# Layer 2's clamp moved from VectorE to GpSimd, its subtraction into a bias on ScalarE, in a four-layer graph network

## The chip, the cores and the metric

The kernel runs on one core of a Trainium2 chip. Its engines are named as in the profile: PE (TensorE, matrix products), DVE (VectorE), ACT (ScalarE), POOL (GpSimd) and SP (SyncE, which only issues transfers here). Each has its own queue and works through it in order; semaphores tie the queues together. The time is the device time of one execution in microseconds, and the lower the better. A profile is one execution on its own, with a span from its first to its last record.

## The reference, cut to what matters

There are 4096 nodes with 64 features and a dense 4096 x 4096 matrix `adj`. Four layers follow each other. Each normalises the rows of `x`, applies relu, aggregates over `adj` in its own way, and adds to `x`. Layer 0 is a plain product, layer 1 attention with a sigmoid, layer 3 a weighting by rank. Layer 2, which is changed, aggregates logarithmic maps on the Poincare ball:

```python
def _logmap(x, y, c):
    sub = _mobius_add(-x, y, c)
    sub_norm = jnp.maximum(jnp.linalg.norm(sub, axis=-1, keepdims=True), MIN_NORM)
    ...
    arg = jnp.clip(sqrt_c * sub_norm, 0.0, TANH_CLIP)
    return 2.0 / (sqrt_c * lam_x) * jnp.arctanh(arg) * sub / sub_norm
...
deg = jnp.maximum(adj.sum(axis=1, keepdims=True), 1e-08)
w = adj / deg
log_ij = _logmap(x[:, None, :], x[None, :, :], c)
agg = jnp.einsum('ij,ijc->ic', w, log_ij)
```

The kernel never forms the 4096 x 4096 x 64 array. For each pair of nodes it computes one number, the hyperbolic distance divided by its hyperbolic sine, multiplies it by `adj`, and sums with a matrix product. With u the scaled hyperbolic cosine that comes out of PE, and SC a power of two that scales it, that number needs u squared less a quarter of SC squared (the squared sine), kept above zero, its square root, its inverse root, and the logarithm of cosine plus root.

## The kernel before, in words

**Tiling.** A work item of layer 2 is a tile of 128 partitions by 2 x 512 elements: two chunks of 128 source nodes against a block of 512 target nodes. The scaled distance is symmetric, so only blocks on and above the diagonal are computed, and blocks above it are also transposed on PE and used a second time ("two"). That makes 72 items in 8 rows of blocks, with 16, 14, 12 and so on down to 2 items; in 8 of the 72, on the diagonal, only half of the tile is needed ("cut"), 128 by 512 elements.

**One item, step by step.** Each step is a generator named `l2_...` (lines 1005 to 1212); the profile's names are those of the tiles.
- `l2_dists` on PE: two float32 products (`mm<-RT,LT`) and two bf16 ones (`mm<-RB,LB`) put u into a PSUM tile. There are two such tiles, so that the distances of item k+2 wait until item k's has been read.
- `l2_squares` on ACT: `v<-mm`, v is u squared.
- `l2_clamps` on DVE: `v<-v`, subtract and keep above a floor, in one instruction with two operations.
- `l2_signs` on PE: a last small product turns u in PSUM into its absolute part.
- `l2_roots` on ACT: Ln of v in place (`v<-v`), Exp with scale 0.5 into t (`t<-v`), Exp with scale -0.5 in place (`v<-v`): root and inverse root.
- `l2_coshs` on DVE: `t<-mm,t`, cosine plus root. This frees the PSUM tile.
- `l2_logs` on ACT: `t<-t`, the second Ln.
- `l2_pairs` on DVE: `t<-t,v`, distance times inverse root.
- `l2_weights` on DVE: `w<-t,adj`; `l2_turns` on PE: `tr<-ident,t`; `l2_weights2` on DVE: `w<-tr,adj`, twice per item.
- `l2_sums` and `l2_sums2` on PE: `acc<-w,HA`, 512 columns wide for the item itself, 256 wide for its transposed use; `l2_gathers` adds the transposed sums into `others`.

The tiles v and t come from one pool of six buffers, so three items can be under way.

**The epilogue of a row.** When a row's last item is summed, `after2` and `before3` (lines 613 and 532) follow for its 512 nodes: two transposes, a product, and some two dozen short instructions on DVE, with copies on ACT, a power on POOL for the norm (`r_nn`), one for the normalisation of layer 3 (`ln_r`), and the addition of a bias on POOL (`x<-x,b`).

**What sets the order.** The order of every queue is fixed when the program is built. `in_turn` (line 712) keeps a set of threads; each offers the engine of its next instruction and the time at which a small model, `Pace` (line 59), thinks that it can start, and the earliest goes next. `Pace.cost` (line 76) prices each instruction. `in_steps` (line 1214) ties several steps to a fixed order: for the item number k of each round it issues its stages one after another, each with an offset ("behind"), so that -1 means the next item and 1 the one before. Layer 2's ACT steps are one such group, its PE steps another, and its DVE steps a third. A changed price moves instructions in all layers, since every thread is planned by the same model.

**The first half of the program** (layers 0 and 1, up to about 482 us) reads `adj` twice, 512 KB at a time, over SP's queue. Layer 0's first products wait for the normalised rows HA, which pass through DVE, ACT, and a power on POOL; between them DVE adds up degrees (`dg<-dg,adj`). Small constants (`later_constants`) are made on POOL and DVE at about 35 to 43 us.

## Time and profile before

| | us |
|---|---|
| median of 3 runs | 1199.96 (1198.93 to 1201.73) |
| the profiled execution | 1194.61 |
| its span | 1192.9 |
| layer 2, about 482 to 957 | 475 |
| PE busy in it | 417.7 |
| DVE busy in it | 435.6 |
| ACT busy in it | 374.2 |
| POOL busy in it | 33.5 |

The profiled execution ran 5.4 us below the median. In the lines of the profile L129 is a helper that records every instruction, so instructions are known by their tiles. A line of a group gives its engine, operation, written tile, read tiles and shape, then the count, the busy time in us and the mean of one in ns, and after the last bar the idle time of that engine just before these instructions and what ended it. A line of the timeline gives start, duration, engine and instruction, with the idle time before it in brackets. A line of the waits gives who waited for whom, us in total, number of times, and the longest. In a table by stretches each engine has its busy time and its instructions, followed by PE's granted clock, the busy share of the transfer engines and GB/s.

### The profile page before, as it was taken

Reading aid. Unit: us, or ns where it says so; the run is one execution under the profiler, and the core shown is the slowest. Engines: PE = TensorE matmul, PEld = TensorE weight load, DVE = VectorE, ACT = ScalarE, POOL = GpSimd, SP = SyncE. Lnnn points to the kernel's source line nnn. Section 1 sums busy time; section 2 is a strip of 40 time slices with the busy share of each in tenths; the row PEclk is TensorE's granted clock in tenths of the full one; section 3 lists DMA queues with packets and bytes.
Section 4 is the critical chain, followed back from the end, with each engine's and each line's share of the span. In section 5 each row is a group of like instructions: output and inputs, shape, how many; then the busy total and the mean of one; then the engine's idle time right before and its main releaser. Section 6 shows DMA issues by size and latency. Waiting matters only on the chain.

```text
span 1192.9 us, 15567 instructions
## 1 busy us (share of the span) xinstructions
PE 1074.0 (90%) x5367; PEld 443.4 (37%) x5392; DVE 954.1 (80%) x1595; ACT 780.4 (65%) x1250; POOL 121.5 (10%) x99
## 2 busy tenths in 40 slices
PE   4799999999999999899979979899879679999997
PEld 1234443333333333244434434344433323333332
DVE  6888888869988988798999999898989884555550
ACT  1055456677767767879888788787877554555554
POOL 3122321102000010000010010100010130000000
PEclk9998999999999999899999999999999889999999
DMA  8899999865767775544535435354444297888830
GB/s 303 290 409 366 400 384 337 301 216 193 246 230 247 254 247 170 194 141 159 194 106 184 169 119 197 108 161 157 159 151 166 94 396 292 316 311 315 308 112 9
DMA packets 77190, 271.75 MB, mean 228 GB/s; under 512 B 10040, under 2 KB 11064, under 8 KB 77112
## 3 DMA queue, kind: packets, MB, share of 16 engines
q1 hardware_dynamic: 75456, 270.57, 63.9%
q8 instruction: 42, 0.69, 0.2%
q10 hardware_dynamic: 1656, 0.20, 0.1%
q14 instruction: 36, 0.29, 0.1%
HBM read 269.68 MB, written 1.05 MB: 227 GB/s over the span
## 4 chain that ended last, share of the span: by engine, by line
PE 48%; DVE 26%; ACT 11%; issue 7%; DMA 5%; POOL 2%; ACTq 0%; SPq 0%; DVEq 0%; POOLq 0%
PE acc L129 23%; PE mm L129 16%; PE tr L129 9%; DVE t L129 6%; DVE w L129 6%; DMA adj<-in_adjT_dram 4%; DVE dg L129 3%; ACT wt L129 3%; ACT v L129 2%; DVE v L129 2%; ACT t L129 1%; DVE sig L129 1%; ACT sig L129 1%; POOL lo_s L129 1%; ACT lo_sq L129 1%
## 5 line engine op out<-in xcount | busy, mean ns | idle before, releaser
L129 PE MATMUL acc<-w,HA 128*65 128x256 f32 (+1 forms) x736 | 251.8, 478 | 32.0 <-DVE w L129 23.7
L129 ACT ACTIVATE v<-v 128x1024 f32<-128x1024 f32 (+1 forms) x144 | 145.3, 1009 | 62.1 <-DVE v L129 59.8
L129 ACT ACTIVATE wt<-mm 128x1024 uint16<-128x1024 f32 x124 | 120.5, 1020 | 98.6 <-PE mm L129 98.6
L129 ACT ACTIVATE sig<-mm,att_b,att_a 128x1024 f32<-128x1024 f32 x128 | 148.3, 1201 | 40.9 <-PE mm L129 39.8
L129 DVE TENSOR_TENSOR sig<-sig,adj 128x1024 f32<-128x1024 f32 x128 | 152.2, 1219 | 25.5 <-ACT sig L129 25.2
L129 PE MATMUL acc<-adj,HA 128*64 128x512 f32 x512 | 128.8, 636 | 25.0 <-DVE HA L129 21.4
L129 DVE TENSOR_TENSOR dg<-dg,adj 128x1024 f32<-128x1024 f32 x114 | 139.1, 1220 | 2.0 <-DMA adj<-in_adjT_dram 0.6
L129 PEld LDWEIGHTS acc<-w,HA 128*65 128x65 f32 x736 | 95.2, 140 | 121.0 <-issue 58.7
L129 PE MATMUL mm<-qT,kT 64*128 64x512 f32 x512 | 129.5, 619 | 3.3 <-ACT sig L129 3.3
L129 PE MATMUL acc<-sig,HL 128*64 128x512 f32 x512 | 123.3, 604 | 1.6 <-DVE sig L129 1.5
L129 PE MATMUL acc<-wt,S 128*64 128x512 bf16 (+1 forms) x479 | 97.5, 388 | 3.0 <-issue 2.7
L129 DVE SCALAR_TENSOR_TENSOR t<-t,v 128x1024 f32<-128x1024 f32 x72 | 83.3, 1157 | 4.1 <-ACT t L129 4.1
L129 DVE SCALAR_TENSOR_TENSOR t<-mm,t 128x1024 f32<-128x1024 f32 x72 | 83.3, 1156 | 3.9 <-ACT t L129 2.1
L129 DVE TENSOR_TENSOR w<-tr,adj 128x512 f32<-128x512 f32 x120 | 78.1, 682 | 8.7 <-PE tr L129 8.7
L129 DVE TENSOR_TENSOR w<-t,adj 128x1024 f32<-128x1024 f32 x72 | 83.5, 1159 | 1.2
L129 PE MATMUL mm<-RT,LT 64*128 64x512 f32 (+1 forms) x288 | 78.8, 624 | 3.6 <-DVE t L129 3.6
L129 PE MATMUL tr<-ident,t 128*128 128x128 f32 x480 | 66.3, 279 | 17.0 <-DVE w L129 7.9
L129 ACT ACTIVATE t<-t 128x1024 f32<-128x1024 f32 x72 | 72.1, 1002 | 13.4 <-DVE t L129 13.2
L129 DVE TENSOR_SCALAR RT<-adj 128x1024 bf16<-128x1024 f32 x74 | 50.0, 689 | 32.2 <-PE mm L129 31.8
L129 ACT ACTIVATE t<-v 128x1024 f32<-128x1024 f32 x72 | 72.7, 1010 | 2.3
L129 PEld LDWEIGHTS mm<-qT,kT 64*128 64x128 f32 x512 | 43.1, 185 | 74.2 <-ACT sig L129 35.2
L129 ACT ACTIVATE v<-mm 128x1024 f32<-128x1024 f32 x72 | 69.2, 962 | 0.8 <-PE mm L129 0.8
(206 smaller groups left out, 1287.3 us busy)
## 6 DMA issues: line engine op xcount, KB each, us to landing
adj<-in_adjT_dram SPq DMA_DIRECT2D x512, 512.0 KB, 4.7
x<-in_x_dram SPq DMA_DIRECT2D x4, 256.0 KB, 4.1
out_dram<-h SPq DMA_DIRECT2D x8, 128.0 KB, 2.5
b<-in_b_dram ACTq DMA_DIRECT2D x2, 32.0 KB, 5.7
W<-in_W_dram ACTq DMA_DIRECT2D x3, 16.0 KB, 3.9
W0T<-in_W0T_dram ACTq DMA_DIRECT2D x2, 16.0 KB, 5.5
W1T<-in_W1T_dram ACTq DMA_DIRECT2D x1, 16.0 KB, 4.9
W1T<-in_b_dram ACTq DMA_DIRECT2D x1, 0.2 KB
```

Of the source, the lines that this page charges most:

```text
L129: done = self.tc.keep_in_program_order(getattr(self.engine, op)(*args, **kw))
```

## The change

The clamp becomes a single maximum on POOL: v is kept at or above the next number over a quarter of SC squared. The subtraction goes into the first logarithm on ACT, as a bias held in a new constant tile `minus`. That logarithm is a step of its own, `l2_first_logs`. ACT's group is put into another order: first logarithm of item k, square of item k+1, the two exponentials of k, second logarithm of k (before, the second logarithm of k-1 came first, and the square of k+1 last). The clamps leave DVE's group and are a thread of their own on POOL. The planner's price of a POOL instruction other than a power or a tiny one changes from 0.3 + n/600 to 0.25 + n/300 us.

```diff
-V_MIN = 2.0**-64
+HALF = 0.25 * SC * SC
...
-            return 1.65 if ALU.pow in kw.values() or n <= 8 else 0.3 + n / 600
+            return 1.65 if ALU.pow in kw.values() or n <= 8 else 0.25 + n / 300
...
+    minus = const.tile([P, 1], F32, name="minus")
+    POOL.memset(minus, -HALF)
...
     def l2_clamps():
         for d in work:
-            yield "DVE", lambda: d.get("square")
+            yield "POOL", lambda: d.get("square")
             v = part(d, d["v"])
-            DVE.tensor_scalar(v, v, -half, V_MIN, ALU.add, ALU.max)
+            POOL.tensor_scalar(v, v, HALF * (1.0 + 2.0**-23), None, ALU.max)
             d["clamped"] = pace.latest
...
+    def l2_first_logs():
+        for d in work:
+            yield "ACT", lambda: latest(d.get("clamped"), opened.get("tables"))
+            v = part(d, d["v"])
+            ACT.activation(v, v, AF.Ln, bias=minus)
+            d["first_log"] = pace.latest
+
     def l2_roots():
         for k, d in enumerate(work):
             yield "ACT", lambda: latest(
-                d.get("clamped"), opened.get("tables"),
+                d.get("first_log"),
                 l1[2 * k + 1 - SIG].get("summed") if 2 * k < SIG else 0.0,
                 ago(work, k, SIG // 2, "weighed"), ago(work, k, SIG // 2, "turned"),
             )
             d["t"] = pair_buffer("t")
+            ACT.activation(part(d, d["t"]), part(d, d["v"]), AF.Exp, scale=0.5)
+            d["root"] = pace.latest
             v = part(d, d["v"])
-            ACT.activation(v, v, AF.Ln)
-            ACT.activation(part(d, d["t"]), v, AF.Exp, scale=0.5)
-            d["root"] = pace.latest
             ACT.activation(v, v, AF.Exp, scale=-0.5)
             d["inverse"] = pace.latest
...
-        in_steps((l2_logs(), 1, once), (l2_roots(), 0, once), (l2_squares(), -1, once)),
         in_steps(
-            (l2_clamps(), 0, once), (l2_pairs(), 1, once), (l2_weights(), 1, once),
+            (l2_first_logs(), 0, once), (l2_squares(), -1, once), (l2_roots(), 0, once), (l2_logs(), 0, once),
+        ),
+        in_steps(
+            (l2_pairs(), 1, once), (l2_weights(), 1, once),
             (l2_coshs(), 0, once), (l2_weights2(), 1, lambda d: 2 if d["two"] else 1 if d["first"] else 0),
         ),
-        l2_gathers(), l3_weights(), l3_pass(), l3_counts(), l3_masks(),
+        l2_clamps(), l2_gathers(), l3_weights(), l3_pass(), l3_counts(), l3_masks(),
```

More of the change, by code (lines that the diff above doesn't have):

```diff
@@ L943, in l1_sums @@
                 follow(with_mark(2, ib, after1(ib, acc, st), before2(ib, st)), ON_S, evicts=True)
-    half = 0.25 * SC * SC
     top = 2.0 * math.atanh(TANH_CLIP)
```

## The prediction

> **What bounds the kernel now.** I read the page's shares, then engine busy time by stretches, then one step of layer 2 in order of time, then the waits.

> ```profile
> span 1192.9 us, 15567 instructions
> PE 1074.0 (90%) x5367; PEld 443.4 (37%) x5392; DVE 954.1 (80%) x1595; ACT 780.4 (65%) x1250; POOL 121.5 (10%) x99
> ```

> PE is busiest and POOL nearly empty. The average mixes three stages; clamps exist only in layer 2, from 482 to about 957 us.

> ```profile
> core 0: us, PE busy (x) PEld busy (x) DVE busy (x) ACT busy (x) POOL busy (x), PEclk, DMA share, GB/s
> 545.00:595.00 50.00, 48.59 (x236) 23.62 (x233) 45.96 (x56) 44.36 (x51) 0.00 (x0) 1.00 0.52 179
> 595.00:625.00 30.00, 24.39 (x109) 11.05 (x108) 27.22 (x46) 23.90 (x29) 4.71 (x3) 0.94 0.33 106
> 770.00:800.00 30.00, 24.89 (x120) 11.38 (x116) 29.09 (x41) 24.07 (x27) 2.17 (x2) 1.00 0.44 145
> ```

> Inside a row of blocks (first stretch) PE is full. Where one row ends and the next begins (the other two) the row's epilogue lands on DVE, and DVE leads: 27.2 and 29.1 of 30 us against PE's 24.4 and 24.9. Over 482 to 957 the same view gives PE 417.7, DVE 435.6, ACT 374.2, POOL 33.5 of 475.0 us. One inner step:

> ```profile
> 565.76 0.68 DVE L129 TENSOR_SCALAR v<-v 128x1024 f32<-128x1024 f32 x1
> 566.48 1.06 ACT L129 ACTIVATE v<-v 128x1024 f32<-128x1024 f32 x1 [0.76 <-DVE v L129]
> 566.60 1.13 PE L129 MATMUL mm<-RT,LT 64*128 64x512 f32 x4
> 567.66 0.40 PE L129 MATMUL mm<-RB,LB 32*128 32x512 bf16 x4
> 567.99 1.94 PE L129 MATMUL acc<-w,HA 128*65 128x256 f32 x8
> 568.75 1.22 DVE L129 SCALAR_TENSOR_TENSOR t<-mm,t 128x1024 f32<-128x1024 f32 x1
> 569.77 1.04 PE L129 MATMUL tr<-ident,t 128*128 128x128 f32 x8
> 570.40 1.29 DVE L129 TENSOR_TENSOR w<-tr,adj 128x512 f32<-128x512 f32 x2 [0.43 <-PE tr L129]
> 570.64 1.88 PE L129 MATMUL acc<-w,HA 128*65 128x512 f32 x4
> 571.61 0.68 DVE L129 TENSOR_SCALAR v<-v 128x1024 f32<-128x1024 f32 x1
> ```

> Clamp to clamp is 5.85 us. PE's pieces follow without a gap: 1.06 + 0.33 + 1.78 + 0.87, and 1.81 for the sum ahead, 5.85. DVE spends 0.43 of it waiting for PE. So a clamp taken off DVE gains nothing in an inner step. The waits show where it can:

> ```profile
> ACT v L129 <- DVE v L129: 59.8, 60, 3.7
> PE acc L129 <- DVE w L129: 23.7, 22, 2.2
> ```

> ACT waits 59.8 us in all for clamps queued behind other DVE work, PE 23.7 us for DVE's weights. The chain of waits holds the clamp (DVE v) for 1.6% of the span, 19 us.

> **Prices.** POOL never ran this operation; the nearest rows, grouped by shape:

> ```profile
> L129 DVE TENSOR_SCALAR v<-v 128x1024 f32<-128x1024 f32 x64 | 43.7, 683 | 7.2 <-ACT v L129 7.2
> L129 POOL TENSOR_TENSOR x<-x,b 128x256 f32<-128x256 f32 x8 | 7.2, 903 | 0.0
> L129 DVE SCALAR_TENSOR_TENSOR hb<-ln_xc,ln_r 128x256 f32<-128x256 f32 x8 | 7.4, 925 | 0.4 <-POOL ln_r L129 0.3
> L129 DVE SCALAR_TENSOR_TENSOR h<-ln_xc,ln_r 128x256 f32<-128x256 f32 x16 | 6.7, 418 | 1.4 <-POOL ln_r L129 1.4
> L129 POOL MEMSET rb<- 128x512 f32 x2 | 1.0, 523 | 0.0
> masks.py:102 POOL TENSOR_SCALAR_AFFINE_SELECT near_f<-near_f 128x128 f32<-128x128 f32 x1 | 0.3, 306 | 0.0
> ```

> A 1-element memset is 0.11 us, so the memset slope is (523-105)/511 = 0.82 ns per element: lower bound 0.11 + 0.84 = 0.95 us for 1024. The one-input select, (306-105)/128 = 1.57 ns, gives 1.7. The two-input add, (903-105)/256 = 3.1 ns, gives 3.3, the upper bound from rows. Spans on POOL are rough[...], and the planner's new price is 3.66 us.

> [...]hb, alongside the POOL add, took 925 ns against 418 for the same shape alone. [...]sigmoid with two took 1201 ns, the relu with none 1020, so about 90 each. I take 1.7 to 2.5 us for the clamp, with 0.95 and 4 as ends.

> **The change, part by part.**

> *Off DVE:* 64 x 0.683 + 8 x 0.414 = 47.0 us. DVE falls from 435.6 to about 389.

> *On ACT:* the first Ln gets a bias pointer, 72 x 0.09 = 6.5 us. No activation is added. The second Ln now follows its own step's two exponentials, and must wait for cosh on DVE (1.22 plus handovers, about 1.4) which only the inverse exponential (1.08) covers: about 0.3 us a step. An ACT loop is then 1.18 + 0.95 + 1.09 + 1.4 + 1.05 = 5.67 us, under PE's 5.85. ACT effectively needs 374 + 6.5 + 20 = 401.

> *On POOL:* 72 clamps, 2 us each 144; with 33.5 of powers and adds, far from full. New wait: square, POOL, first Ln. Between square k+1 and first Ln k+1 ACT runs exponential, inverse, wait, second Ln of k: 1.09 + 1.4 + 1.05 = 3.5 us. That hides the clamp. Behind it on POOL stand the row's powers (2.5 and up to 1.9 us) and the 0.9 add; the exponential of the row's norm on ACT waits for the first.

> [...]DVE's pairs and weights read two SBUF tensors, 2.44 us a step, back to back. By the order of both queues the clamp becomes ready near the weights' end[...] and has 5.85 - 2.44 = 3.4 us before the next pairs.[...]

> *Row changes:* ACT no longer queues behind the epilogue. DVE's 435.6 of 475 was 92% full; with PE's 417.7 the largest and ACT at 401 and DVE at 389 close behind, I fill to 90%: 464, so -11. Ends: 0, and 417.7/0.92 = 454, -21.

> *Start of layer 2:* the eviction of layer 1's last sum now stands ahead of the first Ln, which moves from 484.9 to about 486.3: +1.

> *Layers 0 and 1:* the repriced POOL (and one new memset) reorders the plan. Two more degree adds stand ahead of the first normalised rows on DVE: 2 x 1.22 = 2.4 us later than 12.5, and PE idles until then. The eighth normalisation goes behind the constants: 37.9 becomes about 40.5. Later degree adds come earlier by as much, so I take +1, ends -3 and +5. DMA issue keeps the same 512 loads; layer-2 loads stay in the same pairs, layer 3 does the same work on PE.

> Sum: -11 + 1 + 1 = -9 on the profiled execution's 1194.6 (span 1192.9 and 1.7 around it): 1185.6. The median of the runs lies 5.4 above that execution, so 1191.

> **Rivals.** *B, [...]a slow clamp (slower).* Place: each inner step. Step = 2.44 + clamp. From 3.4 us on it decides. At 3.66 it is 6.10, +0.25 x about 45 inner steps = 11, less 5 at row changes and with the +2 above: 1208. At 4 us the same sum gives 1223. For: the hb row and the two-input slope. Against: one input only. *C, ACT takes the bound over:* row changes add copies of 3.9 us per row to an ACT loop of 5.67, so five steps need 32 where DVE took about 32; gain eaten, 1200. Against: copies can fill the 0.3 us waits. *D, the early reorder persists:* +5 or more through the load-bound start with a small gain in layer 2: 1206. That the clamps stay on DVE is excluded by the queue orders: POOL issues 72 of them.

> **How the numbers follow.** A 0.52, B 0.22, C 0.16, D 0.10. Within 0.2% (2.4 us, about what a measurement of this kernel can tell from none) lie 0.01 of A, 0.02 of B, 0.09 of C: 0.12. Slower: 0.01, 0.18, 0.07, 0.10: 0.36. Faster: 0.50 of A and 0.02 of B: 0.52. Range 1181 (all of the 90-to-92% fill) to 1213 (B up to 3.8 us); A alone 1183 to 1196.

> **What would show it.** Right: clamp spans of 1 to 3 us on POOL, inner steps still 5.85 with PE gapless, ACT's wait for the clamp small, row stretches shorter, pairs and weights still 1.22. Wrong: ACT first Ln waiting for POOL each step; pairs stretched beyond 1.22[...]; step at 2.44 + clamp; first PE matmul well after 15.4 us with the shift still present at 482.

## The result and the profile after

| | before | after |
|---|---|---|
| median of 4 runs, us | 1200.85 (1198.93 to 1202.79) | 1186.58 (1185.22 to 1186.75) |
| the profiled execution, us | 1194.61 | 1186.61 |
| its span, us | 1192.9 | 1184.6 |

The ratio is 0.9879, 95% interval 0.986 to 0.9898: the change makes the kernel 1.2% faster. The predicted time was 1191, its range 1181 to 1213.

The shares on the page of the changed kernel:

```profile
span 1184.6 us, 15638 instructions
...
PE 1078.5 (91%) x5367; PEld 449.7 (38%) x5392; DVE 929.3 (78%) x1523; ACT 783.1 (66%) x1250; POOL 324.3 (27%) x172
```

The 72 clamps have gone from DVE to POOL, which is now busy for 203 us more. DVE, however, lost only 24.9 us (954.1 to 929.3), where the clamps alone were 47.0. The rest is taken up below.

The changed kernel by stretches, the same three as before:

```profile
core 0: us, PE busy (x) PEld busy (x) DVE busy (x) ACT busy (x) POOL busy (x), PEclk, DMA share, GB/s
545.00:595.00 50.00, 50.00 (x245) 24.67 (x245) 43.23 (x49) 45.67 (x50) 23.37 (x10) 1.00 0.54 192
595.00:625.00 30.00, 26.08 (x114) 11.68 (x112) 26.12 (x42) 23.82 (x31) 17.94 (x8) 0.94 0.34 126
770.00:800.00 30.00, 27.30 (x121) 12.68 (x119) 28.16 (x38) 24.17 (x28) 18.50 (x8) 0.94 0.44 154
```

Inside the first row PE is full, as it nearly was. At the two row changes PE is busy for 1.7 and 2.4 us more, and DVE for about 1 us less. In the last stretch the granted clock was 0.94 in the mean, where it had been 1.00 (0.50 from 775.42 to 778.84 us). By busy time times one minus the clock, an estimate from this trace, that is 1.7 of the 2.4 us.

The clamp on POOL and the first logarithm, in the changed kernel's groups by shape:

```profile
L129 POOL TENSOR_SCALAR v<-v 128x1024 f32<-128x1024 f32 x64 | 187.2, 2925 | 194.8 <-ACT v L129 190.4 <-DVE w L129 4.0 <-ACT r_c L129 0.4
...
L129 ACT ACTIVATE v<-v,minus 128x1024 f32<-128x1024 f32 x64 | 72.7, 1137 | 7.8 <-POOL v L129 7.7
```

A clamp takes 2.93 us in the mean, against 0.68 on DVE. ACT waits only 7.7 us for all of them. The waits of the changed kernel, from 482 to 957 us:

```profile
DVE t L129 <- ACT t L129: 44.8, 41, 3.4
...
ACT t L129 <- DVE t L129: 31.3, 51, 2.2
ACT v L129 <- PE mm L129: 30.6, 37, 2.1
...
ACT v L129 <- POOL v L129: 7.7, 11, 1.4
PE acc L129 <- DVE others L129: 7.1, 10, 1.0
PE acc L129 <- DVE w L129: 5.6, 12, 1.3
```

ACT's 59.8 us of waiting for the clamp are gone, and PE's 23.7 us of waiting for weights are 5.6. In their place DVE's cosh waits for ACT's root, ACT's second logarithm for cosh, and ACT's square for PE.

**Where the time went.** Layer 2 can be cut at its squares on ACT (`v<-mm`), one for each item, counted from 0. The differences are taken within one profiled execution each.

| from square to square | before | after | difference |
|---|---|---|---|
| start to 0 (layers 0 and 1) | 482.31 | 482.22 | -0.1 |
| 0 to 16 (first row) | 99.01 | 99.42 | +0.4 |
| row changes: 16-24, 30-36, 42-47, 52-56 | 151.08 | 147.00 | -4.1 |
| inside rows: 24-30, 36-42, 47-52, 56-60 | 126.88 | 131.22 | +4.3 |
| 60 to 71 (short rows, epilogues throughout) | 78.50 | 72.83 | -5.7 |
| 71 to the end (last epilogue, layer 3) | 255.12 | 251.91 | -3.2 |
| sum (span) | | | -8.3 |

So three things happened. The row changes are shorter, 4.1 us in the long rows and 5.7 in the short ones. Inside the rows after the first, steps are longer: items 24 to 30 take 6.12 us each, not 5.90. The end is 3.2 us shorter. Between the first square and the last, layer 2 gained 5.0 us in all (455.5 to 450.5).

### The profile page after: what moved, and what is told of

It is laid out like the page before. It is cut to its first block, busy times and chain, and to the rows that moved or that the text cites. A ratio compares the mean times of both kernels' runs of the same rounds, so it can differ in the third digit from the quotient of the medians.

```text
span 1184.6 us, 15638 instructions
## 1 busy us (share of the span) xinstructions
PE 1078.5 (91%) x5367; PEld 449.7 (38%) x5392; DVE 929.3 (78%) x1523; ACT 783.1 (66%) x1250; POOL 324.3 (27%) x172
## 3 DMA queue, kind: packets, MB, share of 16 engines
HBM read 269.68 MB, written 1.05 MB: 229 GB/s over the span
## 4 chain that ended last, share of the span: by engine, by line
PE 49%; DVE 18%; ACT 11%; issue 10%; POOL 8%; DMA 3%; SPq 0%; ACTq 0%; POOLq 0%; DVEq 0%
PE acc L129 23%; PE mm L129 17%; PE tr L129 8%; DVE dg L129 5%; POOL v L129 4%; ACT wt L129 3%; DVE w L129 3%; ACT v L129 2%; DMA adj<-in_adjT_dram 2%; ACT t L129 2%; DVE t L129 2%; POOL lo_s L129 1%; DVE sig L129 1%; ACT sig L129 1%; POOL ln_r L129 1%
## 5 line engine op out<-in xcount | busy, mean ns | idle before, releaser
L129 PE MATMUL acc<-w,HA 128*65 128x256 f32 (+1 forms) x736 | 256.3, 485 | 13.0 <-DVE others L129 7.1
L129 POOL TENSOR_SCALAR v<-v 128x1024 f32<-128x1024 f32 x72 | 204.8, 2845 | 211.5 <-ACT v L129 205.4
L129 ACT ACTIVATE wt<-mm 128x1024 uint16<-128x1024 f32 x124 | 120.3, 1021 | 94.1 <-PE mm L129 94.1
L129 ACT ACTIVATE sig<-mm,att_b,att_a 128x1024 f32<-128x1024 f32 x128 | 148.3, 1202 | 40.9 <-PE mm L129 39.9
L129 DVE TENSOR_TENSOR sig<-sig,adj 128x1024 f32<-128x1024 f32 x128 | 152.5, 1221 | 25.2 <-ACT sig L129 25.0
L129 PE MATMUL acc<-adj,HA 128*64 128x512 f32 x512 | 128.4, 639 | 24.3 <-DVE HA L129 24.1
L129 DVE TENSOR_TENSOR dg<-dg,adj 128x1024 f32<-128x1024 f32 x114 | 139.2, 1221 | 2.2 <-DMA adj<-in_adjT_dram 0.6
L129 PEld LDWEIGHTS acc<-w,HA 128*65 128x65 f32 x736 | 98.1, 143 | 104.7 <-issue 56.6
L129 PE MATMUL mm<-qT,kT 64*128 64x512 f32 x512 | 129.5, 619 | 3.3 <-ACT sig L129 3.3
L129 PE MATMUL acc<-sig,HL 128*64 128x512 f32 x512 | 123.3, 604 | 1.6 <-DVE sig L129 1.5
L129 DVE SCALAR_TENSOR_TENSOR t<-mm,t 128x1024 f32<-128x1024 f32 x72 | 83.6, 1161 | 44.4 <-ACT t L129 43.9
L129 PE MATMUL acc<-wt,S 128*64 128x512 bf16 (+1 forms) x479 | 97.7, 387 | 3.5 <-issue 2.4
L129 PE MATMUL mm<-RT,LT 64*128 64x512 f32 (+1 forms) x288 | 79.7, 631 | 15.9 <-DVE t L129 15.2
L129 ACT ACTIVATE t<-t 128x1024 f32<-128x1024 f32 x72 | 72.6, 1008 | 31.9 <-DVE t L129 31.3
L129 ACT ACTIVATE v<-mm 128x1024 f32<-128x1024 f32 x72 | 69.8, 970 | 30.7 <-PE mm L129 30.6
L129 POOL TENSOR_TENSOR ln_r<-ln_v,minus_half 128x4 f32<-128x4 f32 x32 | 49.3, 1542 | 148.7 <-DVE ln_v L129 148.7
L129 DVE TENSOR_TENSOR w<-t,adj 128x1024 f32<-128x1024 f32 x72 | 84.0, 1167 | 1.5
L129 DVE SCALAR_TENSOR_TENSOR t<-t,v 128x1024 f32<-128x1024 f32 x72 | 83.7, 1163 | 1.8 <-ACT t L129 0.9
L129 ACT ACTIVATE v<-v,minus 128x1024 f32<-128x1024 f32 x72 | 78.4, 1089 | 7.8 <-POOL v L129 7.7
L129 DVE TENSOR_TENSOR w<-tr,adj 128x512 f32<-128x512 f32 x120 | 77.5, 681 | 1.1 <-PE tr L129 1.1
L129 PE MATMUL tr<-ident,t 128*128 128x128 f32 x480 | 66.1, 280 | 11.9 <-DVE t L129 8.2
L129 DVE TENSOR_SCALAR RT<-adj 128x1024 bf16<-128x1024 f32 x74 | 50.4, 698 | 33.3 <-PE mm L129 33.0
```

Source lines behind the costliest of these rows:

```text
L129: done = self.tc.keep_in_program_order(getattr(self.engine, op)(*args, **kw))
```

## The experiments

Each kernel was timed beside the kernel before on one chip. The ratio is to that kernel.

| run | median, us | kernel before there | ratio (95%) |
|---|---|---|---|
| the change | 1186.58 | 1200.85 | 0.9879 (0.986 to 0.9898) |
| e1, planner's price alone | 1198.04 | 1198.88 | 0.9996 (0.9974 to 1.0017) |
| e2, clamp back on DVE | 1197.02 | 1198.88 | 0.9993 (0.9968 to 1.0017) |
| e3, ACT's old order | 1256.75 (one run) | 1198.88 | |
| e4, POOL in the last rows | 1180.57 | 1198.88 | 0.9862 (0.9817 to 0.9906) |
| e5, split logarithm alone | 1194.09 | 1198.23 | 0.9961 (0.9945 to 0.9976) |
| e6, late order without POOL | 1183.15 | 1198.23 | 0.988 (0.9845 to 0.9915) |
| e7, half a clamp | 1176.90 | 1198.23 | 0.9818 (0.9777 to 0.986) |
| e8, gathers first | 1189.56 | 1198.23 | 0.9931 (0.9902 to 0.996) |
| e9, gathers first in two rows | 1182.43 | 1199.84 | 0.9855 (0.983 to 0.9879) |
| e10, shared clamp | 1220.40 | 1199.84 | 1.0166 (1.0142 to 1.019) |
| e11, shared clamp, gathers first | 1189.27 | 1199.84 | 0.9917 (0.9885 to 0.9948) |
| e12, POOL at row changes | 1180.92 | 1198.20 | 0.9849 (0.9809 to 0.9888) |

And the same cuts, in us, from one profiled execution of each:

| | squares 0 to 60 | 60 to 71 | 71 to the end |
|---|---|---|---|
| before | 376.97 | 78.50 | 255.1 |
| e1 | 379.38 | 79.42 | 258.7 |
| e5 | 373.40 | 79.74 | 256.2 |
| e2 | 385.55 | 75.97 | 251.2 |
| the change | 377.64 | 72.83 | 251.9 |
| e6 | 372.14 | 76.15 | 252.4 |
| e4 | 372.12 | 72.06 | 252.1 |

How far single executions can be trusted shows in kernels that differ in nothing there. From square 16 to square 60, e1 repeats each cut of the kernel before to 0.03 us. The end is another matter: there e1 has the same order as the kernel before on DVE, ACT and POOL, and takes 3.6 us longer. So is the time to the first square, which the table leaves out: it is 4.1 us shorter in e6 than in e5, with the same order up to there.

**e1. Is it only the planner?** The new price moves instructions in every layer, so it was tried alone.

```diff
-            return 1.65 if ALU.pow in kw.values() or n <= 8 else 0.3 + n / 600
+            return 1.65 if ALU.pow in kw.values() or n <= 8 else 0.25 + n / 300
```

> The kernel before with nothing changed but the planner's price of POOL instructions (0.25 + n/300 in place of 0.3 + n/600). Replanning theory: a good part of the 14 us comes from the other places that the repriced plan gives to instructions of all layers, so 1187 to 1194. Last-rows theory (the gain is the clamp leaving DVE where the epilogue of a short row and the clamp meet, in the sixth row change and after): no gain here, within 3 us of the kernel before, first PE product again about 3.7 us late and caught up by 52 us.

1198.04, ratio 0.9996. The price alone brings nothing. The replanning theory falls.

**e2. Is it POOL, or ACT's new order?** The maximum goes back to DVE, ahead of the pairs; ACT keeps the new order and the bias.

```diff
-            yield "POOL", lambda: d.get("square")
+            yield "DVE", lambda: d.get("square")
...
-            POOL.tensor_scalar(v, v, HALF * (1.0 + 2.0**-23), None, ALU.max)
+            DVE.tensor_scalar(v, v, HALF * (1.0 + 2.0**-23), None, ALU.max)
...
+            (l2_clamps(), 0, once),
             (l2_pairs(), 1, once), (l2_weights(), 1, once),
```

> The changed kernel with the maximum put back on DVE, ahead of the pairs, and everything else kept (ACT's new order, the bias). Order theory (the gain comes from the second logarithm in its own step, POOL is beside the point): 1185 to 1189. Last-rows theory: POOL is what gains, so the time goes back to 1199 or more, since the new order's longer steps in the middle rows stay: 1199 to 1208, and the stretch from the square of item 67 to that of item 71 is back near 30 us.

1197.02, ratio 0.9993. With this order on ACT in all rows, POOL is what gains: the ratio goes from 0.9993 to 0.9879. Its waits, from 482 to 957 us, have the old entry back:

```profile
ACT v L129 <- DVE v L129: 57.6, 59, 2.2
```

The expectation was half wrong in place, though. Items 66 to 70 took 25.15 us, as in the changed kernel (24.96) and not near the 26.95 of before: there the new order alone gains. In the first 60 items the new order with the clamp on DVE loses 8.6 us against before, and POOL wins 7.9 of that back.

**e3. Is the new order needed?** The clamp stays on POOL, and ACT gets its old order back.

```diff
-            (l2_first_logs(), 0, once), (l2_squares(), -1, once), (l2_roots(), 0, once), (l2_logs(), 0, once),
+            (l2_logs(), 1, once), (l2_first_logs(), 0, once), (l2_roots(), 0, once), (l2_squares(), -1, once),
```

> The changed kernel with ACT's order of before (second logarithm of the item before, first logarithm, two exponentials, square of the next item), clamp still on POOL. Between the square and the first logarithm of an item ACT then has only one second logarithm, 1.05 us, against a clamp of 2.8 us and two handovers of about 0.1: 1.9 us are bare in each step. An ACT loop of 1.05 + 1.14 + 1.07 + 1.06 + 0.95 + 1.9 = 7.2 us takes the place of 5.85 to 6.1: +1.1 to +1.35 us in some 60 steps, 1250 to 1270. If the clamp is hidden by other engines' slack instead, the time stays at 1187.

1256.75, in the expected band. One step in order of time, ACT and POOL alone:

```profile
646.02 1.01 ACT L129 ACTIVATE v<-mm 128x1024 f32<-128x1024 f32 x1
...
646.92 1.05 ACT L129 ACTIVATE t<-t 128x1024 f32<-128x1024 f32 x1
647.11 2.77 POOL L129 TENSOR_SCALAR v<-v 128x1024 f32<-128x1024 f32 x1 [4.36 <-ACT v L129]
...
649.90 1.15 ACT L129 ACTIVATE v<-v,minus 128x1024 f32<-128x1024 f32 x1 [1.94 <-POOL v L129]
```

ACT stands for 1.94 us before the logarithm, and the step is 649.90 - 642.78 (the logarithm before) = 7.12 us. A clamp of 2.8 us is hidden in an inner step only because the order puts two exponentials and a logarithm between square and first logarithm.

**e5, e4, e6. Which rows gain, and from what?** In e5 all clamps are on DVE and ACT has its old order; only the first logarithm is a step of its own, with the bias. In e4 the last 12 items (rows five to seven, counted from 0) have POOL and the new order as well. In e6 these 12 have the new order with the clamp on DVE. The edit of e4; e5 has 8 in place of 5, and e6 keeps every clamp on DVE:

```diff
+    POOL_FROM = 5
+    def early_items(d):
+        return 1 if d["ib"] < POOL_FROM else 0
...
+            (l2_logs(early_items), 1, early_items), (l2_first_logs(), 0, once),
+            (l2_squares(late_items), -1, late_items), (l2_roots(), 0, once),
+            (l2_logs(late_items), 0, late_items), (l2_squares(early_items), -1, early_items),
...
+            (l2_clamps("DVE"), 0, early_items),
...
+        l2_clamps("POOL"), l2_gathers(), l3_weights(), l3_pass(), l3_counts(), l3_masks(),
```

> All clamps on DVE, ACT's old order in all rows, but the first logarithm as a step of its own with the bias, as in the changed kernel, so that copies of the epilogue can go between it and the exponentials. Split theory (this is what made the first 52 items of the run with POOL in the last rows 5.4 us shorter): 1188 to 1194. Late theory (all of that run's 18 us come from POOL and the new order in the last 12 items and from what follows them): 1196 to 1200.

> The clamps of the first five rows (60 items) stay on DVE in ACT's old order; only the last 12 items use POOL and the new order. Last-rows theory: the whole gain is there, and the middle rows get their steps of 5.90 back: 1183 to 1189, the stretch between the squares of items 67 and 71 at 25 to 26 us. Spread theory (each row change gives a part of the gain, and the longer steps take it back): about a seventh to a third of the gain is left, 1196 to 1199.

> As the run with POOL in the last rows, but with the clamps of the last 12 items on DVE as well: POOL does nothing new, only ACT's order changes for them. Order theory for the short rows (the second logarithm in its own step is the gain there; with the clamp on DVE throughout the new order brought items 66 to 70 from 27.9 to 25.2 us): 1180 to 1184, as fast as with POOL. Offload theory (DVE must be rid of the clamp there): 1188 to 1196.

e5 gives 1194.09, e6 1183.15, e4 1180.57. The split alone is worth about 0.4%. In the profiled executions 6.0 us lie in the first 60 items (379.38 to 373.40 us from e1 to e5, with steps of 5.85 in place of 5.90). Why it helps was not followed further. From e5 to e6 only the order of the last 12 items changes, and the ratio falls from 0.9961 to 0.988: 1.3 us up to square 60, whose own place the new order already moves, 3.6 us between squares 60 and 71, and 3.8 us after. From e6 to e4 POOL takes these 12 clamps: 4.1 us between squares 60 and 71, mostly in items 70 to 71 (9.44 to 6.48, the same two times as in e2 and the change). But the two ratios overlap, so what this last part is worth in the whole time is not settled.

Between squares 60 and 71, then, order and POOL bring about as much each: 2.5 and 3.1 us from before by way of e2 to the change, 3.6 and 4.1 us from e5 by way of e6 to e4. My theory that the clamp's departure from DVE explains the short rows does not hold on its own. And e6, which has every clamp on DVE, is as fast as the change (0.988 and 0.9879): a gain of this size does not need POOL.

e4 leaves POOL out of 60 of 72 items and is not slower than the change. In its first 60 items it beats the change by 5.5 us, though 1.3 of them are the place of square 60 again (e5 has 373.40). Its steps inside rows are not lengthened: items 24 to 30 took 35.09 us.

**e7. Does the length of POOL's clamp matter?** POOL clamps one chunk of two. The other half stays unclamped, and the bias is halved.

```diff
             v = part(d, d["v"])
+            v = v if d["cut"] else v[:, 0:1, :]
             POOL.tensor_scalar(v, v, HALF * (1.0 + 2.0**-23), None, ALU.max)
```

> The changed kernel with POOL's maximum over one of the two chunks only (the other is left as it is, with half the bias so that the logarithm stays defined): about 1.5 us in place of 2.8 to 3.0. Hidden-clamp theory (the first logarithm waits for the second logarithm ahead of it on ACT, the clamp ends about 0.2 us before): no change in inner steps, 1183 to 1188. Clamp-on-the-path theory (the chain of waits holds POOL's clamp for 4%, 47 us): half of it goes, 1165 to 1178.

1176.90, ratio 0.9818, where the hidden-clamp theory allowed no less than 1183. It matters, but not in every inner step: items 24 to 30 took 36.95 us (36.71 in the changed kernel). Between the first and the last square 11.6 us are gained in the profiled executions: 3.3 at the row changes of the long rows, 3.4 inside these rows behind them, and 2.5 each in the first row and in the short rows. The second row change of the changed kernel, by stretches:

```profile
694.00:698.00 4.00, 2.38 (x9) 0.67 (x6) 3.22 (x8) 2.21 (x3) 3.57 (x2) 1.00 0.39 135
698.00:700.00 2.00, 1.35 (x8) 0.40 (x8) 1.97 (x5) 1.37 (x3) 0.00 (x0) 1.00 0.00 0
700.00:704.00 4.00, 3.47 (x13) 1.94 (x10) 3.93 (x6) 3.94 (x4) 2.74 (x2) 0.57 0.00 0
```

and of the kernel with half a clamp, 7 us earlier:

```profile
687.00:691.00 4.00, 2.73 (x12) 1.03 (x10) 3.76 (x8) 2.37 (x4) 1.85 (x1) 1.00 0.41 135
691.00:693.00 2.00, 1.46 (x8) 0.40 (x8) 1.97 (x5) 1.82 (x3) 0.00 (x0) 1.00 0.00 0
693.00:697.00 4.00, 3.72 (x18) 2.21 (x19) 3.93 (x7) 3.67 (x5) 3.26 (x2) 1.00 0.00 0
```

PE's longest pause there is 2.11 us in the first and 1.30 in the second, and only after the first does the granted clock fall (0.57 against 1.00 in the last line). A count over stretches of 1 us between squares 0 and 71 divides PE's time into idle time, busy time lost to the clock (estimated as busy time times one minus the granted clock) and the rest, counted as work at full clock:

| us, squares 0 to 71 | all | idle | lost to the clock | work |
|---|---|---|---|---|
| before | 456 | 52.1 | 10.1 | 393.7 |
| the change | 451 | 41.7 | 15.5 | 393.8 |
| e7, half a clamp | 439 | 40.8 | 3.2 | 395.1 |

Half a clamp leaves the idle time nearly as it is. In these two executions the clock accounts, by this estimate, for all that it gained here, but e7's is the fastest of its four runs (1171.58 of 1171.58 to 1179.70), and run by run clock and time go together only loosely: one run of e7 took 1178.66 us at a mean granted clock of 0.983, while the change took 1186.55 at 0.981 and 1186.61 at 0.976. So the clock is not shown to be the whole of the gain. Why it held was not separated: with the shorter clamp the pauses at row changes are shorter, and so are POOL's powers (last section).

**e8, e9. What lengthened the steps inside rows?** From the second row on, DVE adds the transposed sums into `others`, once in two steps. In the changed kernel the planner put this between pairs and weights:

```profile
648.21 1.22 DVE L129 SCALAR_TENSOR_TENSOR t<-t,v 128x1024 f32<-128x1024 f32 x1
...
649.35 0.68 DVE L129 TENSOR_TENSOR others<-acc,others 65x512 f32<-65x512 f32 x1
...
649.95 1.21 DVE L129 TENSOR_TENSOR w<-t,adj 128x1024 f32<-128x1024 f32 x1
...
650.17 1.91 PE L129 MATMUL acc<-w,HA 128*65 128x256 f32 x8 [0.51 <-DVE others L129]
```

PE waits 0.51 us for it, what follows on PE is late, and so are the next distances and the next square, which in the new order stands ahead of the exponentials (at 643.85, in the step before these lines, the square had waited 1.12 us for PE). Before the change the gather stood between cosh and the turned weights. e8 puts it ahead of the pairs, in all rows but the first; e9 in the second and third row alone. The edit of e9; in e8 all rows but the first are meant by `ahead`:

```diff
+            (l2_gathers(True), 3, lambda d: int(d["two"] and d["half"] == 1 and ahead(d))),
             (l2_pairs(), 1, once), (l2_weights(), 1, once),
```

> The changed kernel with the gathers of the rows after the first put in DVE's order ahead of the pairs instead of wherever the planner lets them fall. Gather theory (the 6.12 us steps of the second row come from PE's transposed sums waiting for a gather that stands between pairs and weights): items 24 to 30 back at 5.85 to 5.90 a step, about 36 such steps shorter by 0.25, 1176 to 1181. If the new order of ACT itself (square ahead of the exponentials) sets 6.12, nothing changes: 1185 to 1189.

> The changed kernel with the gathers ahead of the pairs in the second and third row only; all other rows and the end as the planner lays them. Gather theory: items 24 to 30 and 36 to 42 take 35.1 us each (36.7 and 36.3 in the changed kernel), the last rows keep their gain (70 to 71 near 6.5 us, not 12.3), so 3 to 4.5 us less than the changed kernel: 1182 to 1184. Against it: if what is won there is lost at the next row change, 1186 to 1188.

e8 gave 1189.56, outside both bands, but its steps are as the gather theory has them: items 24 to 30 took 35.09 us and 36 to 42 took 35.08, or 5.85 each. Its steps in order of time, DVE and PE:

```profile
647.73 0.68 DVE L129 TENSOR_TENSOR others<-acc,others 65x512 f32<-65x512 f32 x1
...
647.74 1.13 PE L129 MATMUL mm<-RT,LT 64*128 64x512 f32 x4
648.32 1.21 DVE L129 SCALAR_TENSOR_TENSOR t<-t,v 128x1024 f32<-128x1024 f32 x1
...
648.80 0.39 PE L129 MATMUL mm<-RB,LB 32*128 32x512 bf16 x4
...
649.13 1.94 PE L129 MATMUL acc<-w,HA 128*65 128x256 f32 x8
```

PE goes on without a pause. The fixed place costs elsewhere: items 70 to 71 took 12.29 us in e8 (6.47 in the changed kernel). Nor does it help in the fourth and fifth row: 47 to 52 took 31.13 us (31.24), and 56 to 60 took 28.15 (26.97), as in e9 (28.17), which leaves those rows to the planner. e9 keeps clear of the end: items 24 to 30 at 35.08, 70 to 71 at 6.48, 1182.43 us. Items 36 to 42 came only from 36.31 to 35.92. So the gather's place is the cause of the longer steps in the second row, and of part of those in the third; in the fourth and fifth e8 does not bear it out, and what lengthens their steps stays open. e9's ratio overlaps the change's.

**e10, e11. Can the clamp be shared?** POOL takes one chunk, DVE the other: in e10 DVE's half goes wherever the planner puts it, in e11 between weights and cosh, with e9's gathers.

```diff
-        l2_clamps(), l2_gathers(), l3_weights(), l3_pass(), l3_counts(), l3_masks(),
+        l2_clamps("POOL", 0), l2_clamps("DVE", 1), l2_gathers(), l3_weights(), l3_pass(), l3_counts(), l3_masks(),
```

> The changed kernel with the maximum of one chunk on POOL and of the other on DVE, so that the whole is done and POOL's part takes 1.5 us in place of 2.8. Clamp-length theory (POOL's clamp is bare at row changes, and half of it gave 9.7 us): 1176 to 1181, row changes 1 to 1.6 us shorter as with half a clamp. Queue theory (what gains is that no part of the clamp stands behind the epilogue on DVE; the maximum wholly on DVE gave 1197): the row changes go back to the times with the clamp on DVE, 1188 to 1197.

> The shared clamp, its DVE half in a fixed place between weights and cosh, with the gathers of the second and third row ahead of the pairs. If both causes are right and apart, 1172 to 1178, items 24 to 30 and 36 to 42 at 35.1 us. If the fixed place puts the DVE half behind the epilogue at row changes, 1185 to 1195.

e10 is slower than before, at 1220.40 us and outside both bands. In its groups the first logarithm shows why:

```profile
L129 ACT ACTIVATE v<-v,minus 128x1024 f32<-128x1024 f32 x72 | 78.5, 1090 | 31.8 <-DVE v L129 31.5
```

ACT waits 31.5 us for DVE's half, up to 6.3 us at a time by the waits: 0.56 us of work in the mean, in DVE's queue where the planner puts it, costs more than 2.8 us on POOL. With a fixed place (e11) this wait is gone, but the time is 1189.27; its items 24 to 30 and 36 to 42 took 34.88 and 35.01, and it loses in the last rows (60 to 71 in 75.79 us).

**e12. Both orders, each where it gains.** e4, with POOL and the new order also in the first six items of the second to fifth row.

```diff
     def early_items(d):
-        return 1 if d["ib"] < POOL_FROM else 0
+        return 1 if d["ib"] == 0 or d["ib"] < 5 and place_in_row[id(d)] >= 6 else 0
```

> The kernel with POOL and the new order in the last 12 items, with both now also in the first six items of the second to fifth row, where the epilogue of the row before is under way; DVE and the old order in the rest. Theory of two effects (POOL gains 0.5 to 2 us at a row change, the new order loses 0.2 us a step inside a row): items 16 to 24 at 50, 30 to 36 at 39 to 39.5, 42 to 47 at 32 to 32.5 us, items 24 to 30 and 36 to 42 still at 35.1, so 3 to 5 us under that kernel at the last square: 1175 to 1178. If the switch back to the old order leaves its step bare each time (a DVE clamp between square and first logarithm, 1.2 to 1.5 us), the gain is eaten: 1180 to 1183.

1180.92, the second band. Whole rows compared (a square's place in the step differs where the order switches): 16 to 30 in 84.53 us (e4 86.18), 30 to 42 in 74.45 (74.90), 42 to 52 in 62.96 (63.21), but 52 to 60 in 51.66 (49.89) and 60 to 66 in 42.50 (40.34). What the longer rows gain, the next ones lose. No complete version was shown to beat the change: e4, e9 and e12 have medians 4 to 6 us lower and ratios that overlap its own.

## Why the prediction was right, point by point

**The clamp's price.** Taken as 1.7 to 2.5 us, measured 2.77 with nothing beside it and 2.93 in the mean: too low. The two-input slope of the bounds, 3.3 us, was nearer than the memset and select slopes. The clamp took four times DVE's 0.68 us. 2.77 lies under the 3.4 us from which rival B decides, and B did not come. B's sum, 2.44 + clamp, was the author's estimate from the `hb` row: it has the clamp and DVE's pairs and weights one after the other. The traces do not show that throughout: at 512.43 us of the changed kernel a clamp took 2.76 us with the whole 1.22 us of the weights beside it.

**Off DVE.** 47.0 us left, but DVE's busy time fell by 24.9 only. Group by group, 16 us came back as longer DVE instructions; the other 6 are instructions that overlapped the clamps and were counted once. The two groups that grew most belong to the epilogue. In the kernel before:

```profile
L129 DVE TENSOR_TENSOR hb<-hb,S 128x256 f32<-128x256 f32 x8 | 3.3, 412 | 1.2 <-ACT S L129 1.2
...
L129 DVE TENSOR_SCALAR r_c<-r_c 128x4 f32<-128x4 f32 x16 | 2.7, 169 | 3.8 <-ACT r_c L129 3.5
```

and in the changed kernel:

```profile
L129 DVE TENSOR_TENSOR hb<-hb,S 128x256 f32<-128x256 f32 x8 | 6.7, 840 | 0.5 <-ACT S L129 0.5
L129 DVE TENSOR_SCALAR r_c<-r_c 128x4 f32<-128x4 f32 x16 | 6.4, 397 | 2.9 <-ACT r_c L129 2.6
```

With the clamp on DVE (e2) they are back at 414 and 169 ns. Where they grew, a clamp was running: at the second row change one began at 694.80 and `r_c` took 0.77 us from 695.09; another began at 709.23 and `hb` took 1.26 from 709.33. The prediction looked for longer instructions only at pairs and weights; those stayed at 1.22 and 1.23 us in the mean, and the clamps beside them were longer instead. Of the 27 clamps of full width that ran beside them for 0.35 us or more, 24 took 2.98 to 3.92 us and three 2.76 to 2.77; the 29 that met none of them took 2.76 to 2.77. At `r_c` and `hb` the added time was less than the clamp's: the longest `r_c` took 1.00 us and the longest `hb` 1.26, beside clamps of 2.80 to 3.14. `hb` reads two tensors there, `r_c` one. What makes one of the two engines wait for the other was not shown.

**On ACT.** The bias pointer costs 1137 - 1056 = 81 ns. The 90 of the prediction were an estimate: half of the 181 ns by which sigmoid, with two such pointers, is longer than relu, with none (1201 and 1020 ns). The second logarithm waits 31.3 us for cosh, 0.43 a step, where 0.3 was taken. ACT did not become the bound.

**The clamp is hidden, inner steps stay at 5.85.** Right for the first row (5.85, PE gapless), and the order is what hides it (e3). Wrong from the second row on: 6.12, +4.3 us in all. The step that failed is the one that costs the order at nothing inside a row. It counted engines one by one and left out the gather on DVE, whose place the planner chooses anew: that is the cause in the second row and partly in the third (e8, e9), and the rest stays open.

**Row changes, -11.** -4.1 and -5.7 make -9.8, so the size is right at this place. As a forecast of all of layer 2, for which the sum used it, it was twice too large: -5.0 between the first and the last square, since the steps inside rows grew. The reason given ("ACT no longer queues behind the epilogue") is right for the long rows, by e2 (151.20 us there with the clamp on DVE, 147.00 on POOL). It is incomplete for the short ones, where the new order brings about half (e6).

**Start of layer 2, +1.** The square of item 10 comes at 546.60 before and 546.56 after: nothing is left.

**Layers 0 and 1, +1.** The first product on PE came 3.7 us later (12.99 to 16.70; 2.4 predicted), and the shift was down to 0.4 us by 52 us. The first square came 0.1 us earlier.

**The end.** Not in the sum. It is 3.2 us shorter. e2 and e6, with the clamp on DVE, are as short there (251.2 and 252.4), and the three kernels of the table with the old order are not (255.1 to 258.7), so this seems to belong to the new order. But two executions with one order were 3.6 us apart there.

**The sum.** 1194.6 - 9 = 1185.6 for the profiled execution, which took 1186.61. That they agree to 1 us is luck, for the terms missed cancel: +4.3 inside rows, +1.2 at the row changes and +0.4 in the first row, against -3.2 at the end and -1 each at the two starts. The further 5.4 us, from the profiled execution to the median, did not carry over: the changed kernel's profile lies at its own median. That is why the sum met 1186.58 and the forecast of 1191, though inside its range, was 4.4 us too high.

## What to carry to other kernels

In this kernel, work taken off an engine that queues behind a burst gained at the burst and nowhere else. It could cost four times as much on the slower engine (2.77 us, 0.68 before), since the order kept enough independent work between its input and its reader (e3 shows the loss without that). But try the order alone as well: in the last rows, with the split logarithm, it brought as much as the whole change, and no clamp was moved (e6). Look then at what a new order does to the instructions that it doesn't name: here longer steps, at least partly from one short addition that the planner moved, took back almost half of what the row changes gave. Compare stages and whole rows, since gains and losses of 4 to 6 us had nearly cancelled in the long rows and would have read as no effect.

## What the hardware showed unexpectedly

**The granted clock after a pause of PE.** The kernel before, by stretches of 2 us around its last but one row change:

```profile
927.00:929.00 2.00, 0.00 (x0) 0.00 (x0) 1.35 (x3) 1.17 (x3) 1.65 (x1) 0.98 0.60 215
929.00:931.00 2.00, 0.00 (x0) 0.00 (x0) 1.76 (x7) 1.74 (x2) 0.00 (x0) 0.50 0.37 145
931.00:933.00 2.00, 1.66 (x5) 1.15 (x6) 1.54 (x4) 0.42 (x1) 0.00 (x0) 0.50 0.00 0
933.00:935.00 2.00, 2.00 (x4) 0.47 (x2) 1.97 (x5) 0.65 (x1) 1.14 (x1) 0.50 0.00 0
935.00:937.00 2.00, 2.00 (x11) 0.59 (x10) 2.00 (x3) 1.94 (x3) 1.03 (x2) 0.82 0.00 0
```

PE pauses for 5.08 us from 926.26, and the granted clock is 0.50 for 6.8 us (928.9 to 935.7), more than 4 of them after PE has work again.

In two cases it mattered where a pause fell. The kernel before has one of 2.22 us at 695.36 and one of 2.21 us at 834.61. By the steps of its grid:

```profile
693.39:696.80 3.41, 1.97 (x10) 0.40 (x8) 2.76 (x9) 2.06 (x3) 0.11 (x1) 1.00 0.37 143
696.80:700.21 3.41, 2.23 (x11) 1.34 (x12) 3.38 (x7) 1.91 (x3) 2.01 (x2) 1.00 0.00 0
833.34:836.75 3.41, 1.27 (x8) 0.21 (x7) 3.17 (x10) 1.92 (x3) 0.00 (x0) 1.00 0.19 76
836.75:840.16 3.41, 3.33 (x8) 1.90 (x9) 3.38 (x7) 2.17 (x3) 2.17 (x2) 0.50 0.00 0
```

The first pause is split between two steps, with 1.97 and 2.23 us of PE's work in them, and the clock stays at 1.00. The second lies in one, which leaves PE 1.27 us of work in it, and the clock is 0.50 in the next. What the clock takes also differs between executions of one kernel: e2's twelve runs had mean granted clocks of 0.971 (1202.77 us) to 0.987 (1193.12 us).

A pause at a row change can so come with more than its length: after the one of 5.08 us PE did 4.39 us of work at 0.50, by the estimate of e7 a loss of 2.2 us. The prediction had no term for it. By the table in e7, in these two executions the change took 10.4 us of idle time from PE between the first and the last square, and the clock took 5.4 us of it back. No run tried the clock by itself.

**POOL's power and DVE.** The power of the row's norm (`r_nn`, 128 x 8) took 1.67 us in one place and 2.72 in another of the same kernel. At 692.10 us of the changed kernel it took 2.72, having begun 0.03 us after DVE's pairs; with half a clamp it began 0.10 us ahead of them and took 1.67. At the next two row changes of the changed kernel (768.18 and 832.00 us) it began 0.03 us after the pairs again and took 2.72, and with half a clamp it took 1.67 there (759.71 and 821.78); at the first of the changed kernel it began 0.03 us ahead and took 1.67. Starts 0.06 to 0.13 us apart against the pairs' went with 1.05 us in the epilogue. No run tried this alone.
